# Two of four score heads are turned by SBUF to SBUF DMAs instead of by way of DRAM, and the loads around them change places

## The chip, the cores and the metric

The kernel runs on one core of a Trainium2 chip. The time is the device time in microseconds; before the change its median is 3578.6 us over three runs (3576.97 to 3579.74). The engines are named as in the profile: PE multiplies matrices, PEld loads its weights, DVE, ACT and POOL work on tiles, and SP issues the DMAs.

## The reference, cut to what matters

A Perceiver layer of three blocks, 16 sequences of 128 queries each with 512 features, in float32. Only the first block touches the change: cross attention of 16 heads of 32 features over a context of 2048 rows.

```python
q = queries @ wq.T + bq
k = context @ wk.T + bk
v = context @ wv.T + bv
attn = jnp.einsum('bhnd,bhsd->bhns', q, k) * scale
attn = jax.nn.softmax(attn, axis=-1)
out = jnp.einsum('bhns,bhsd->bhnd', attn, v)
out = out.transpose(0, 2, 1, 3).reshape(B, NQ, D)
return out @ wo.T + bo
```

Behind it come a Mamba block (projections, a causal convolution, a state scan over 16 states, a gated output and an MLP) and a mixture of experts.

## The kernel before, in words

The order of the work is written out by hand: each engine, and SP's queue with it, takes its instructions in the order of the program. The main loop runs over steps u. One step of the first 256 handles one sequence b, one block of 512 context rows and one group of four heads: u = 16 b + 4 block + group. Beside that, each step carries a piece of the projections of the next block and, from u = 54 on, a piece of the Mamba scan of sequences already attended to. Four steps make one block, 32 steps one cycle of the Mamba part (two sequences).

**Scores and their turning.** `scores(u)` writes four banks of PSUM (L307), `maxima` (L315, DVE) and `exps` (L325, ACT) turn them into the tile `pr`. The product with the values needs the probabilities turned. Two of the four heads are turned by PE with an identity (`turn`, L357, copied out by ACT in L359). The other two are turned by DVE and DMAs: `blocks(u)` transposes 32 x 32 blocks into the tile `tr` (L337, one buffer) and writes it to a DRAM tile `trd` with one DMA (L341). In the next step `gathered` reads it back with four DMAs, one for each 32 partitions of the tile `pd` (L347, one buffer), so that the blocks end up in their places. `weighted` (L385) multiplies the PE-turned heads of step u - 1 and the DMA-turned heads of step u - 2 in step u.

**Keys and values.** The projections of the context are made by a scheme with seven products in place of eight. The context block lies in four quarters, loaded by `load_ctx` (L158): `c00`, `c01`, `c10`, `c11`. POOL makes four differences of them in `ctx_sums` (L236): t1 = c01 - c00, t2 = c11 - t1, t3 = c11 - c01, t4 = c10 - t2. The products (L244) run over the four steps before a block is needed: keys with u % 4 = 1 and 2, values with u % 4 = 3 and 0. In the steps with u % 4 = 1 and 3 the products are: first with c00 and c10 (`x_products`, at the head of the step), later with t2 (`y_products`, at its end). In the steps with u % 4 = 2 and 0: first with t3 and t1, later with t4 and c11. The differences are made at u % 4 = 1, t1 and t2 first. c01 has one buffer, the other quarters two; c00, c10 and c11 of the next block are loaded at u % 4 = 1, c01 at u % 4 = 2.

**SP's queue.** All loads and stores of the loop are issued by SP. In a step its order is: the four reads of `gathered` for the step before; `step_loads` (loads of x and others, and the next but one B); the write of `tr`; `later_loads` (the next C, then the weights of the Mamba and output projections, then the context quarters). B and C are rows of `bcd` broadcast to all partitions (`load_bc`, L647), each with two buffers; POOL multiplies B in (`inputs`, L698) a step ahead, and POOL and DVE multiply C in (`scan`, L735).

**The step size of the Mamba part.** `dt_second` computes e = u - 1 - e on DVE (L679) and the logarithm of u on ACT into a tile `l` of its own (L681); POOL uses it a step later (L687).

Of the kernel before, what the change touches and what calls it, by code (L numbers as in the profile page):

```python
# [8 lines left out]
FP = mybir.dt.float32  # L9
AF = mybir.ActivationFunctionType  # L10
# [5 lines left out]
P = 128  # L16
B, NQ, D, S = 16, 128, 512, 2048
H, HD = 16, 32
KC = D // P
SB = S // 512  # L20
DI, DS, DTR = 1024, 16, 32
# [4 lines left out]
GT = GB * NQ  # L26
# [5 lines left out]
ND = 2  # L32
# [4 lines left out]
def perceiver_layer(ctx: ExitStack, tc: tile.TileContext, a: dict, out: bass.AP):  # L37
    nc = tc.nc
# [19 lines left out]
    zd = [dram.tile([NQ, D], FP, tag=f"zd{b}", name=f"zd{b}") for b in range(B)]  # L58
    xnd = [dram.tile([NQ, D], FP, tag=f"xnd{b}", name=f"xnd{b}") for b in range(B)]
    bcd = [dram.tile([2 * DS, GT], FP, tag=f"bcd{g}", name=f"bcd{g}") for g in range(B // GB)]  # L60

    trd = [dram.tile([P, ND * 512], FP, tag=f"trd{i}", name=f"trd{i}") for i in range(2)]

    mv = const.tile([P, B, 2], FP, tag="mv", name="mv")
    rstd = const.tile([P, B], FP, tag="rstd", name="rstd")
# [44 lines left out]
    LAG = 22  # L110
    Z_GATES = (20, 22, 25, 34, 36, 38, 40, 50)
    NF = B // MB
    with ExitStack() as es:
# [37 lines left out]
        def load_ctx(g, names=("c00", "c10", "c11", "c01")):  # L151

            for n in names:
                j, c = int(n[1]), int(n[2])
                t = pool.tile(
                    [P, 2, 256], FP, tag=n, name=f"{n}_{g}", bufs=1 if n == "c01" else 2
                )
                nc.sync.dma_start(  # L158
                    t,
                    a["ctxT"][g // SB, g % SB][  # L160
                        :, 2 * j : 2 * j + 2, c * 256 : (c + 1) * 256
                    ],
                )
                ctx_t[g, j, c] = t
# [60 lines left out]
        def ctx_sums(g, names):  # L225
            b11, b12, b21, b22 = (ctx_t[g, j, c] for j in range(2) for c in range(2))
            for n in names:
                t = pool.tile([P, 2, 256], FP, tag=n, name=f"{n}_{g}", bufs=1)
                cfac[g, n] = t
                x, y = {  # L230
                    "t1": lambda: (b12, b11),
                    "t2": lambda: (b22, cfac[g, "t1"]),
                    "t3": lambda: (b22, b12),
                    "t4": lambda: (b21, cfac[g, "t2"]),
                }[n]()
                nc.gpsimd.tensor_tensor(t, x, y, ALU.subtract)  # L236
# [97 lines left out]
        def blocks(u):  # L334

            t = pool.tile([P, 4, ND, 4, 32], FP, tag="tr", name=f"tr{u}", bufs=1)
            nc.vector.transpose(  # L337
                t.rearrange("p c h i q -> p (h i) c q"),
                prs[u][:, NP:, :].rearrange("p h (i c k) -> p (h i) c k", i=4, c=4),
            )  # L340
            nc.sync.dma_start(trd[u % 2], t.rearrange("p c h i q -> p (c h i q)"))  # L341

        def gathered(u):

            pd = pool.tile([P, 4, ND, 4, 32], FP, tag="pd", name=f"pd{u}", bufs=1)
            for c in range(4):
                nc.sync.dma_start(  # L347
                    pd[c * 32 : (c + 1) * 32].rearrange("k a h i q -> k a (h i q)"),
                    trd[u % 2].rearrange("(a k) (c r) -> c k a r", k=32, c=4)[c],
                )  # L350
            pds[u] = pd

        def turn(u, j):
# [323 lines left out]
        def dt_second(g, ec):  # L677
            dt, e, u = dts[g, ec]
            nc.vector.scalar_tensor_tensor(e, u, 1.0, e, ALU.subtract, ALU.subtract)  # L679
            l = ssm.tile([P, GT], FP, tag="l", name="l", bufs=1)  # L680
            nc.scalar.activation(l, u, AF.Ln)  # L681
            dts[g, ec] = dt, e, l

        def dt_third(g, ec):
            dt, e, u = dts[g, ec]
# [643 lines left out]
        for u in range(last):  # L1329
            live = u < NU  # L1330
            g, r = divmod(u - 32 - LAG, 32)
            scans = 0 <= g < NG

            made, phase = divmod(u + 3, 4)
            makes = 0 < made < B * SB
            of, phase = ("k", "v")[phase // 2], phase % 2

            def step_loads():
                for f in loads.get(u, ()):
                    f()  # L1340
                load_bc(u + 2 - 32 - LAG, 0)

            def later_loads():
                load_bc(u + 1 - 32 - LAG, DS)
                for f in weights.get(u, ()):
                    f()
                if u % 4 == 1 and made + 1 < B * SB:
                    load_ctx(made + 1, ("c00", "c10", "c11"))
                if u % 4 == 2 and made + 1 < B * SB:
                    load_ctx(made + 1, ("c01",))  # L1350

            if not 1 <= u <= NU:
                step_loads()
            if u > NU:
                later_loads()
            if scans and u <= NU:
                decays(g, r, 0)
            if u > NU:
                while fed < feeds * (u - NU) // (last - 1 - NU):
                    feed(fed)  # L1360
                    fed += 1
                if scans:
                    decays(g, r, 0)
            if u == NU + 1:
                load_rows()
            if live:
                scores(u)
            if 1 <= u <= NU:
                weighted(u - 1, range(4))
                if u > 1:  # L1370
                    weighted_last(u - 2)
                weighted_out(u - 1)
                gathered(u - 1)
                step_loads()
            for f in early.get(u, ()):
                f()
            if u == NU:
                weighted(NU, range(NP, 4))
                weighted_last(u - 1)
                att.close()  # L1380
                give_back(*banks, flat(avp))
                open_ffn()
            if u == NU + 8:
                load_wex()
            for f in head.get(u, ()):
                f()
            if live:
                maxima(u)
            if makes:
                x_products(of, made, phase, pa, pc)  # L1390
            if live:
                exps(u)

            turns = ("t1", "t2", "t3", "t4") if u % 16 == 5 else ("t1", "t2")
            if makes and u % 4 == 1:
                ctx_sums(made, turns)
            for f in between.get(u, ()):
                f()
            if 0 <= u + 1 - 32 - LAG < 32 * NG:
                inputs(*divmod(u + 1 - 32 - LAG, 32))  # L1400
            if makes and u % 4 == 1 and len(turns) == 2:
                ctx_sums(made, ("t3", "t4"))
            silu_third()
            if scans:
                scan(g, r, 0)
            if live and u % 4 == 2:
                values_kept(u // 4)
            if makes:
                hold(of, made, pa, "u1")
            if scans:  # L1410
                decays(g, r, 1)
            if live:
                blocks(u)
            if makes:
                x_sums(of, made, phase, pa, pc)
            if u <= NU:
                later_loads()

            after_turns = late.get(u, ())
            free = banks[NP:]
            places = [(free + banks)[i] for i in range(len(after_turns))]
            if live and len(after_turns) > len(free):
                if u % 4 == 0:
                    places = [flat(avp), *places[:-1]]
                elif u % 2 and makes and u not in behind:
                    places[-1] = flat(pc)

            ahead = live and u % 16 in (3, 10) and len(after_turns) == 1  # L1430
            if ahead:
                after_turns[0](free[0])
                after_turns, places = (), ()
            if live:
                for j in range(NP):
                    turn(u, j)
            if scans and not (live and u % 2):
                scan(g, r, 1)
            for f in middle.get(u, ()):
                f()  # L1440
            for f, ps in zip(after_turns, places):
                if live:
                    f(ps)
                else:
                    ps = bank()
                    f(ps)
                    give_back(ps)
            if scans and live and u % 2:
                scan(g, r, 1)
            for f in after.get(u, ()):  # L1450
                f()
            for f in inner.get(u, ()):
                f()
            if makes:
                y_products(of, made, phase, pa, pc)
                y_sums(of, made, phase, pa, pc)
            for f in behind.get(u, ()):
                ps = flat(pc) if makes else banks[2] if live else bank()
                f(ps)
                if not live:  # L1460
                    give_back(ps)
            silu_second()
# [76 lines left out]
```

## Time and profile before

| What | Value |
|---|---|
| median of three runs | 3578.6 us |
| the profiled execution's own time | 3579.3 us |
| its span, first to last instruction | 3577.5 us |
| granted TensorE clock, mean | 0.995 |
| PE busy | 3518.9 us, 98% |
| DVE, POOL, ACT busy | 2672.0, 2462.7, 2285.5 us |
| DMA engines' share, 200 to 400 us | 0.47 |
| DMA engines' share, 1100 to 2800 us | 0.79 |

In the profile, "busy" is the time in which an engine executes. A list of waits gives, for each kind of instruction, the time in which its engine stood idle before it and whose work ended that idling. SP has no busy time; each of its rows is the issuing of a DMA, and the time "to landing" runs from the start of the issue until the data is there. In the timeline a row has its start, its length, the engine, the line of the kernel, the operation and the tiles written and read; x4 stands for four merged instructions.

### The profile page before, as it was taken

Reading aid. Unit: us, or ns where it says so; the run is one execution under the profiler, and the core shown is the slowest. Engines: PE = TensorE matmul, PEld = TensorE weight load, DVE = VectorE, ACT = ScalarE, POOL = GpSimd, SP = SyncE. Lnnn points to the kernel's source line nnn. Section 1 sums busy time; section 2 is a strip of 40 time slices with the busy share of each in tenths; the row PEclk is TensorE's granted clock in tenths of the full one; section 3 lists DMA queues with packets and bytes.
Section 4 is the critical chain, followed back from the end, with each engine's and each line's share of the span. In section 5 each row is a group of like instructions: output and inputs, shape, how many; then the busy total and the mean of one; then the engine's idle time right before and its main releaser. Section 6 shows DMA issues by size and latency. Waiting matters only on the chain.

```text
span 3577.5 us, 68547 instructions
## 1 busy us (share of the span) xinstructions
PE 3518.9 (98%) x24072; PEld 2638.5 (74%) x24072; DVE 2672.0 (75%) x4390; ACT 2285.5 (64%) x5672; POOL 2462.7 (69%) x2353
## 2 busy tenths in 40 slices
PE   8999999999999999999999999999999989999999
PEld 6777787778777877787778777877777756656655
DVE  4555556897889788978797879887988767668743
ACT  3555556777677766777677767776777665545422
POOL 2111214896889788978797779777987778789920
PEclk9999999999999999999999999999999999999999
DMA  4444445787788778787788778778777887676742
GB/s 146 159 148 154 159 152 193 250 265 220 254 251 268 233 253 256 252 243 247 250 257 247 231 257 265 240 224 271 254 245 224 266 300 254 219 273 245 260 173 77
DMA packets 527541, 816.79 MB, mean 228 GB/s; under 512 B 44848, under 2 KB 378960, under 8 KB 526944
## 3 DMA queue, kind: packets, MB, share of 16 engines
q1 hardware_dynamic: 526752, 811.79, 70.4%
q8 instruction: 192, 3.15, 0.3%
q14 instruction: 149, 1.22, 0.1%
q0 software_dynamic: 448, 0.63, 0.1%
HBM read 661.51 MB, written 150.73 MB: 227 GB/s over the span
## 4 chain that ended last, share of the span: by engine, by line
PE 86%; DVE 4%; POOL 4%; DMA 3%; ACT 3%; issue 1%; SPq 0%; DVEq 0%; POOLq 0%
PE pa L244 24%; PE pc L244 17%; PE bank L307 7%; PE avp L385 7%; PE bank L577 6%; PE bank L357 6%; PE bank L986 3%; PE bank L762 3%; PE bank L955 2%; PE bank L1087 2%; PE bank L515 2%; ACT pr L325 1%; POOL w L698 1%; DMA bc<-bcd 1%; PE bank L442 1%
## 5 line engine op out<-in xcount | busy, mean ns | idle before, releaser
L325 ACT ACTIVATE pr<-bank,nm 128x512 f32<-128x512 f32 x1024 | 688.5, 684 | 199.3 <-DVE nm L315 197.3
L315 DVE TENSOR_REDUCE nm<-bank 128x1 f32<-128x512 f32 x1024 | 633.8, 678 | 60.0 <-PE bank L307 59.6
L698 POOL TENSOR_TENSOR w<-dx,bc 128x512 f32<-128x512 f32 x512 | 648.1, 1287 | 30.7 <-DMA bc<-bcd 22.6
L749 POOL TENSOR_TENSOR ysum<-ysum,w 128x512 f32<-128x512 f32 x384 | 500.4, 1303 | 229.4 <-DVE hst L712 205.9
L719 ACT ACTIVATE hst<-dt,alog 128x254 f32<-128x254 f32 x918 | 442.4, 482 | 71.5 <-DVE hst L712 39.1
L337 DVE STREAM_TRANSPOSE tr<-pr 128x1024 f32<-128x1024 f32 x256 | 318.8, 1245 | 119.9 <-ACT pr L325 110.3
L735 POOL TENSOR_TENSOR w<-w,bc 128x512 f32<-128x512 f32 x256 | 329.1, 1286 | 76.6 <-DVE w L734 74.0
L385 PEld LDWEIGHTS avp<-pT,v 128*32 128x32 f32 x4096 | 204.4, 110 | 198.3 <-issue 194.2
L734 DVE TENSOR_TENSOR_SCAN w<-hst,w 128x512 f32<-128x512 f32 x256 | 309.5, 1209 | 40.0 <-ACT hst L719 33.2
L236 POOL TENSOR_TENSOR t<-c,c 128x512 f32<-128x512 f32 x128 | 164.3, 1283 | 232.3 <-PE pc L244 135.6
L359 ACT COPY pT<-bank 128x512 f32<-128x512 f32 x512 | 271.7, 581 | 48.9 <-PE bank L357 48.8
L307 PE MATMUL bank<-kt,qT 32*128 32x512 f32 x2048 | 301.3, 641 | 1.6 <-ACT pT L359 1.6
L385 PE MATMUL avp<-pT,v 128*32 128x128 f32 x4096 | 276.4, 277 | 1.5 <-ACT pT L359 1.4
L357 PE MATMUL bank<-ident,pr 128*128 128x128 f32 x2048 | 266.2, 273 | 0.8 <-ACT pr L325 0.7
L357 PEld LDWEIGHTS bank<-ident,pr 128*128 128x128 f32 x2048 | 239.1, 141 | 27.7 <-ACT pr L325 2.5
L734 DVE TENSOR_TENSOR_SCAN hst<-hst,w 128x512 f32<-128x512 f32 x203 | 247.8, 1221 | 7.1 <-ACT hst L719 7.1
L244 PE MATMUL pa<-t,ks 128*128 128x256 f32 x1024 | 248.6, 386 | 0.0
L244 PE MATMUL pa<-vs,t 128*128 128x256 f32 x1008 | 244.8, 386 | 0.0
L577 PE MATMUL bank<-zT,win 128*128 128x256 f32 x992 | 224.8, 379 | 0.0
L244 PEld LDWEIGHTS pa<-t,ks 128*128 128x128 f32 x1024 | 185.9, 190 | 36.0 <-issue 13.8
L244 PEld LDWEIGHTS pa<-vs,t 128*128 128x128 f32 x1008 | 183.0, 190 | 35.6 <-ACT hst L719 9.9
L385 PE MATMUL avp<-pd,v 128*32 128x128 f32 x3072 | 205.8, 276 | 3.2 <-DMA pd<-trd 3.2
(315 smaller groups left out, 7709.8 us busy)
## 6 DMA issues: line engine op xcount, KB each, us to landing
bc<-bcd SPq DMA_DIRECT2D x512, 512.0 KB, 5.3
trd<-tr SPq DMA_DIRECT2D x256, 512.0 KB, 3.8
pd<-trd SPq DMA_DIRECT2D x1024, 128.0 KB, 2.9
c<-in_ctxT_dram SPq DMA_DIRECT2D x256, 256.0 KB, 6.0
wf<-in_w_dram SPq DMA_DIRECT2D x124, 512.0 KB, 6.7
wqo<-in_wqkvo_dram SPq DMA_DIRECT2D x128, 256.0 KB, 6.3
win<-in_win_dram SPq DMA_DIRECT2D x128, 256.0 KB, 5.9
wout<-in_wout_dram SPq DMA_DIRECT2D x128, 256.0 KB, 6.2
```

The costliest lines, as they stand in the source:

```text
L244: nc.tensor.matmul(ps[:, r, :], l[:, kc, r * P : (r + 1) * P], m[:, kc, :], start=(i in (1, 2, 5) and r == 0 and kc == 0), stop=(r == 1 an ...
L307: nc.tensor.matmul(banks[j], qts[b][rows, hg, :], kts[u // 4, hg][rows, :], start=True, stop=True)
L315: nc.vector.tensor_reduce(stats[b][0][j][:, sb, hg : hg + 1], banks[j], AX.X, ALU.max, negate=True)
L325: nc.scalar.activation(pr[:, j, :], banks[j], AF.Exp, bias=nm[j][:, sb, hg : hg + 1], accum_out=sm[:, sb, h : h + 1],)
L357: nc.tensor.transpose(ps[:, i, :], prs[u][:, j, i * P : (i + 1) * P], ident)
L385: nc.tensor.matmul(avp[j * HD : (j + 1) * HD, v % 4, :], values(v, i, j), pts[v, j][:, i, :] if j < NP else pds[v][:, :, j - NP, i, :], st ...
L577: nc.tensor.matmul(ps, w[:, kc, :], zTs[g][:, kc, :], start=(kc == 0), stop=(kc == KC - 1))
L698: nc.gpsimd.tensor_tensor(w, dx.unsqueeze(1).to_broadcast([P, NH // 2, GT]), bcs[g * 32 + r, 0][:, i * NH // 2 : (i + 1) * NH // 2, :], AL ...
L719: nc.scalar.activation(bt(h[:, k, :])[:, :, 1:], bt(dt)[:, :, 1:], AF.Exp, scale=aneg[:, ec, n : n + 1],)
L734: nc.vector.tensor_tensor_scan(y if i else x, y, x, 0.0, ALU.mult, ALU.add)
L735: eng.tensor_tensor(w, to, bcs[g * 32 + r, DS][:, i * NH // 2 : (i + 1) * NH // 2, :], ALU.mult)
L749: nc.gpsimd.tensor_tensor(s, s, w, ALU.add)
```

## The change

In `blocks(u)`, right behind the transposes, sixteen DMAs now move `tr` into `pd` within SBUF: for each of four 32-partition blocks of the source (a) and each of four of the destination (c) one DMA of 32 rows of 1 KB. `gathered` and the DRAM tiles are gone. `pd` has two buffers.

The loads change places. C is asked for in `step_loads`, right after B, ahead of the sixteen. Of the context quarters only c11 keeps two buffers. t3 is written in place over c01. c01 of the next block is asked for at u % 4 = 0, c11 at u % 4 = 1, c00 and c10 at u % 4 = 3; all behind the sixteen and behind the weights of the step.

In `dt_second` the logarithm is written over u; the tile `l` is gone.

```diff
-    trd = [dram.tile([P, ND * 512], FP, tag=f"trd{i}", name=f"trd{i}") for i in range(2)]
...
-                    [P, 2, 256], FP, tag=n, name=f"{n}_{g}", bufs=1 if n == "c01" else 2
+                    [P, 2, 256], FP, tag=n, name=f"{n}_{g}", bufs=2 if n == "c11" else 1
...
             for n in names:
-                t = pool.tile([P, 2, 256], FP, tag=n, name=f"{n}_{g}", bufs=1)
+                if n == "t3":
+                    t = b12
+                else:
+                    t = pool.tile([P, 2, 256], FP, tag=n, name=f"{n}_{g}", bufs=1)
...
-            nc.sync.dma_start(trd[u % 2], t.rearrange("p c h i q -> p (c h i q)"))
-
-        def gathered(u):
-
-            pd = pool.tile([P, 4, ND, 4, 32], FP, tag="pd", name=f"pd{u}", bufs=1)
-            for c in range(4):
-                nc.sync.dma_start(
-                    pd[c * 32 : (c + 1) * 32].rearrange("k a h i q -> k a (h i q)"),
-                    trd[u % 2].rearrange("(a k) (c r) -> c k a r", k=32, c=4)[c],
-                )
+            pd = pool.tile([P, 4, ND, 4, 32], FP, tag="pd", name=f"pd{u}", bufs=2)
+            for a_ in range(4):
+                for c in range(4):
+                    nc.sync.dma_start(
+                        pd[c * 32 : (c + 1) * 32, a_].rearrange("k h i q -> k (h i q)"),
+                        t[a_ * 32 : (a_ + 1) * 32, c].rearrange("k h i q -> k (h i q)"),
+                    )
             pds[u] = pd
...
-            l = ssm.tile([P, GT], FP, tag="l", name="l", bufs=1)
-            nc.scalar.activation(l, u, AF.Ln)
-            dts[g, ec] = dt, e, l
+            nc.scalar.activation(u, u, AF.Ln)
+            dts[g, ec] = dt, e, u
...
                 load_bc(u + 2 - 32 - LAG, 0)
+                load_bc(u + 1 - 32 - LAG, DS)
...
             def later_loads():
-                load_bc(u + 1 - 32 - LAG, DS)
                 for f in weights.get(u, ()):
                     f()
-                if u % 4 == 1 and made + 1 < B * SB:
-                    load_ctx(made + 1, ("c00", "c10", "c11"))
-                if u % 4 == 2 and made + 1 < B * SB:
-                    load_ctx(made + 1, ("c01",))
+                names = (("c01",), ("c11",), (), ("c00", "c10"))[u % 4]
+                if u and made + 1 < B * SB:
+                    load_ctx(made + 1, names)
...
                 weighted_out(u - 1)
-                gathered(u - 1)
                 step_loads()
```

## The prediction, made before the changed kernel was run

> **What bounds the kernel now.** I read the page first: the busy shares, then PE's waits, then SP's own waits, and last the timeline of one step, because the change lies wholly on SP's queue.
>
> ```profile
> span 3577.5 us, 68547 instructions
> ...
> PE 3518.9 (98%) x24072; PEld 2638.5 (74%) x24072; DVE 2672.0 (75%) x4390; ACT 2285.5 (64%) x5672; POOL 2462.7 (69%) x2353
> ...
> pd<-trd SPq DMA_DIRECT2D x1024, 128.0 KB, 2.9
> c<-in_ctxT_dram SPq DMA_DIRECT2D x256, 256.0 KB, 6.0
> ```
>
> PE is busy for 98% and idles 59 us; a change that takes no matmul away can gain a part of that at most. The next fence is PE's list of waits, in us in total, times, longest.
>
> ```profile
> PE bank L432 <- ACT pr L325: 7.8, 6, 1.4
> PE avp L385 <- DMA pd<-trd: 6.5, 3, 3.2
> PE bank L631 <- POOL xa L625: 4.7, 6, 0.8
> ```
>
> So the transfers that the change replaces cost PE 6.5 us in all, in three places: 2.9 and 3.2 us in the last steps, 0.3 us at 1093. The rest of PE's waits the change doesn't touch. Now SP's own waits:
>
> ```profile
> SPq L341 <- DMA c<-in_ctxT_dram: 23.5, 35, 1.3
> SPq L647 <- DMA c<-in_ctxT_dram: 34.6, 49, 1.4
> ```
>
> The write of `tr` (L341) and the loads of B and C (L647) use nothing of the context, yet wait for context loads. The semaphores of SP's DMAs show why: eight take turns, and a DMA is not issued until the one eight places earlier has landed. The timeline shows a step (u = 96, scores at 1062.75) and the next:
>
> ```profile
> 1062.75 1.14 PE L307 MATMUL bank<-kt,qT 32*128 32x512 f32 x8
> ...
> 1068.31 1.25 DVE L337 STREAM_TRANSPOSE tr<-pr 128x1024 f32<-128x1024 f32 x1 [0.43 <-ACT pr L325]
> ...
> 1070.02 0.38 SPq L341 DMA_DIRECT2D trd<-tr  x1
> ...
> 1070.44 0.43 SPq L647 DMA_DIRECT2D bc<-bcd  x1
> ...
> 1072.81 1.14 PE L307 MATMUL bank<-kt,qT 32*128 32x512 f32 x8
> ...
> 1073.55 1.28 POOL L236 TENSOR_TENSOR t<-c,c 128x512 f32<-128x512 f32 x1
> ...
> 1074.90 1.27 POOL L236 TENSOR_TENSOR t<-c,t 128x512 f32<-128x512 f32 x1
> ...
> 1076.48 1.74 SPq L347 DMA_DIRECT2D pd<-trd  x4
> ...
> 1079.33 1.89 PE L244 MATMUL pa<-t,ks 128*128 128x256 f32 x8
> ```
>
> Two things are to be seen. Four DMAs back to back take 1.74 us; a lone issue is 0.32 and the median 0.43, so one follows another every 0.475 us. And the quarter c01 has a short chain behind it: POOL makes t1 from it, t2 from t1 (1076.17), and PE wants t2 at 1079.33, in that same step.
>
> **Part 1: sixteen DMAs for five.** Gone are the 512 KB write (0.34 us of SP) and four reads (1.74). Sixteen of 32 KB come, 16 x 0.475 = 7.6 us. SP is taken 5.5 us longer a step, where a step is (2888.1 - 43.1)/256 = 11.1 us; with B and C (0.95) and the other loads (about 1.8 from the issues' medians) it is taken for 10.3. The pitch is bounded below by the shortest issue of L347 plus the gap, 0.302 + 0.043 = 0.345. Above, it is landing over eight: the other 32-row DMA, dtw, lands in 5.1 us at the median, so 0.64. I take 0.475, the nearest row: dtw too has a median issue of 0.43, so fewer rows don't shorten it. What follows in later_loads is pushed behind the sixteen.
>
> At the end the two pd waits go, since pd is asked for a step earlier: -6 us; next late there are ACT's copies (0.24 us at 2874.73, 1.4 at 2897.88). In the steps before, pd has a whole step more and stays hidden. PE has to wait for eight semaphores in place of four: its EVENT_SEMAPHORE is 51 ns, so 0 to 256 x 4 x 0.05 = 52 us; I take 0, as they are read while eight score matmuls (1.07 us) run.
>
> **Part 2: c01 asked for one step ahead.** Before, it was asked for at u % 4 = 2, three steps ahead. Now t3 lies in its buffer until PE has read it at u % 4 = 0, and only then, behind the sixteen and the step's weights, is c01 loaded, for t1 in the next step. In the step shown the transposes end at 1069.56; the sixteen take until 1077.16; c01 lands 3.6 us later; t1 and t2 take 2.62; t2 stands at 1083.4 and PE wanted it at 1079.33. PE stalls 4.0 us. The landing is bounded by 2.9 (the shortest of the context loads) and 6.0 (their median); I take 3.6, near the short end, because the sixteen ahead are small and the 512 KB write and its reading are gone.
>
> From the end of the transposes to t2 is thus 7.6 + 3.6 + 2.6 = 13.8 us, plus weights ahead of c01: four wo (2.0), two win (1.5), eight wout (4.0). The time until PE wants t2 I read from eight such timelines, u % 32 = 0, 4, 8 ... 28: 9.8, 10.9, 13.4, 20.3, 11.8, 10.7, 16.4, 13.3. With weights 0, 2, 1.5, 1.5, 0, 2, 4, 0 the stalls are 4.0, 4.9, 1.9, 0, 2.0, 5.1, 1.4, 0.5: 19.8 us a cycle, and 50 groups make 6.25 cycles: **124 us**. The thirteen groups before u = 56 (9.8 to 10.6 us in eight, 13.2 and more in five) give **38 us**. POOL, 82% busy between 1062 and 1428, waits with PE; it had run ahead of PE and I charge nothing more.
>
> **Part 3: one `tr` buffer, read by sixteen DMAs.** The next transposes wait until the last has landed. From one to the next: 15 x 0.475 + 2.4 (shortest landing of L347) + 1.25 + some 0.1 = 10.9 us. Steps 2 to 39 last 9.7: 38 x 1.2 = 46 us, of which part 2 already stalls 31, so 15 more. In the cycle from u = 91 to 104 fourteen steps take 140.7 us against 152.6, part 2 stalls 9.4 there, 2.5 remain, 16 us over 6.25 cycles. Together **31 us**; with a landing of 2.0 nearly nothing, with 3.6 see the second rival.
>
> **Part 4: eight in flight.** Eight issues are 3.8 us, wout lands in 6.2: a burst of weights holds the queue 2.4 us. About two a cycle fall ahead of a c01 (u % 32 = 22 and 24): some 5.5 us a cycle, **35 us**; none if landing shortens, 110 if every group has one.
>
> **Parts at nothing.** C is asked for before the sixteen; its buffer is free at the latest 6.1 us into a step (POOL's L735 at u % 32 = 6 and 22), when the transposes end too: SP would have waited for those. c11 and two single quarters come two steps or more ahead. Ln in place now waits for DVE's L679, 1.95 us in most of 64 cases; behind it on ACT a copy of v ends 1.1 us before PE reads it and moves into that margin. Cover gone, it is 64 x 1.95 = 125 us; but ACT idles 36% and c01's stall comes later in the same chain, so 0.
>
> The Trainium skill, "DMA: Bandwidth & Descriptors", section "Rules for kernel authors", speaks against the change: coalesce small transfers, since under 64 KB one pays mostly overhead. [...] The row of four issues in 1.74 us that land 2.9 us after issue shows that they overlap, so the sum goes by 0.475.
>
> **Sum.** 124 + 38 + 31 + 35 - 6 = 222 us on the profiled execution's 3579.3 (span 3577.5; 0.7 above the median 3578.6): 3801, said as 3800.
>
> **Rivals.** *The loop of part 3 binds every step.* With a landing of 3.6 and a pitch of 0.5 it is 7.5 + 3.6 + 1.4 = 12.5 us; 256 x (12.5 - 11.1) = 355, and c01's stall is swallowed: 3930. For it: context loads land in 6.0. Against: DMA engines lose the 512 KB write, and are at 0.79 in the middle.
> *The mild one.* Pitch 0.345, landing 2.9: 11.0 in place of 13.8; the stalls are 1.2, 2.1 and 2.3 a cycle, 35 us, and 13 before u = 56; less 6: 3621. Against it: 732 back-to-back pairs at 0.43.
> *Not slower.* c01 is there in time, and only the pd waits go: 3573. It decides at u % 32 = 0: sixteen pitches and a landing must fit 9.8 - 2.6 = 7.2 us, with 2.9 a pitch of 0.27. No issue of L347 is that short.
>
> **How the numbers follow.** Forecast 0.60 (3680 to 3900), loop 0.16, mild 0.13, not slower 0.11. The range 3600 to 3930 leaves out the last and half the loop's, 0.19. A measurement here can tell 0.2%, 7 us: the last case splits into same 0.07 and faster 0.04; slower 0.89.
>
> **What would show it.** PE waits before L244 `t,ks` for POOL L236, some 2 to 5 us at u % 4 = 1; L236 waits for DMA of `c`; SP's sixteen take 7 to 8 us; DVE's L337 waits for DMAs; no pd wait in PE's list. Wrong if sixteen issues take under 4.5 us, or if t1 starts as early as before.

## The result: 4664 us, and the profile after

The changed kernel takes 4663.7 us (median of four runs, 4663.1 to 4670.7) against 3577.9 us before (3577.0 to 3579.7). The ratio is 1.304, with a 95% interval of 1.302 to 1.306. The direction was forecast, the size was not: +1086 us where +222 had been worked out and 3930 was the range's end.

The page of the changed kernel: the span, the busy times (us, share, instructions), the chain of work that ended last, and three rows of the DMA issues (KB each, median us to landing).

```profile
span 4661.2 us, 72193 instructions
...
PE 3829.9 (82%) x24072; PEld 2785.7 (60%) x24072; DVE 2658.2 (57%) x4390; ACT 2296.2 (49%) x5672; POOL 2456.9 (53%) x2353
...
PE 34%; SPq 22%; DMA 20%; POOL 10%; issue 7%; DVE 5%; ACT 2%; DVEq 0%; POOLq 0%
...
bc<-bcd SPq DMA_DIRECT2D x512, 512.0 KB, 6.0
pd<-tr SPq DMA_DIRECT2D x4096, 32.0 KB, 1.9
c<-in_ctxT_dram SPq DMA_DIRECT2D x256, 256.0 KB, 3.4
```

PE idles 831 us (4661.2 - 3829.9) where it idled 59: 773 us more. Its busy time, for the same 24072 matmuls, is 311 us longer (3829.9 - 3518.9). Together that is the whole growth of the span, 1084 us. In the chain SP's queue and the DMAs hold 42%; before, PE alone held 86%, in the chain of that page:

```profile
PE 86%; DVE 4%; POOL 4%; DMA 3%; ACT 3%; issue 1%; SPq 0%; DVEq 0%; POOLq 0%
```

The single transfer is not slow: the moves land 1.9 us after their issue, the context quarters 3.4 us in place of 6.0.

PE's own list of waits in the changed kernel (us in total, times, longest us):

```profile
PE pa L245 <- POOL t L237: 349.5, 54, 13.5
PE pc L245 <- DVE v L275: 110.3, 35, 8.8
...
PE avp L383 <- DMA pd<-tr: 13.9, 5, 6.2
```

The products wait for POOL's differences. The list of waits of all engines says what POOL and DVE wait for:

```profile
POOL t L237 <- DMA c<-in_ctxT_dram: 792.6, 36, 64.8
DVE tr L338 <- DMA pd<-tr: 601.0, 137, 10.3
```

Both are waits for DMAs that SP issued late. SP's queue, in the timeline (start, length, issues merged under x16 and x4), over some 50 us (u = 100 to 102):

```profile
1502.03 13.00 SPq L345 DMA_DIRECT2D pd<-tr  x16
1515.08 2.00 SPq L171 DMA_DIRECT2D wqo<-in_wqkvo_dram  x4
1517.18 0.38 SPq L156 DMA_DIRECT2D c<-in_ctxT_dram  x1
1517.65 0.89 SPq L645 DMA_DIRECT2D bc<-bcd  x2
1518.64 12.73 SPq L345 DMA_DIRECT2D pd<-tr  x16
...
1535.64 10.45 SPq L345 DMA_DIRECT2D pd<-tr  x16
```

There is hardly a hole in that queue, and the sixteen moves take 10.5 to 13.0 us of a step, not 7.6. The same stretch in the timeline of the other engines shows what hangs on it: the transposes had waited for the last burst, and the quarter of the block, which stands in the queue at 1517.18, lets POOL start at 1522.31 and PE at 1524.96.

```profile
1500.72 1.25 DVE L338 STREAM_TRANSPOSE tr<-pr 128x1024 f32<-128x1024 f32 x1 [5.10 <-DMA pd<-tr]
...
1522.31 1.26 POOL L237 TENSOR_TENSOR t<-c,c 128x512 f32<-128x512 f32 x1 [13.66 <-DMA c<-in_ctxT_dram]
...
1524.96 3.78 PE L245 MATMUL pa<-t,ks 128*128 128x256 f32 x8 [11.82 <-POOL t L237]
```

The last row has a second thing in it: those eight matmuls take 3.78 us, where the eight of the step shown of before took 1.89. They run at half clock (granted clock 0.5) after 11.8 us of idling.

One issue's price is in the views by line: the moves of the changed kernel, and the four reads that they replace in the kernel before (ns minimum / median / maximum, first and last start).

```profile
L345 SPq DMA_DIRECT2D pd<-tr x4096: 507/588/2047, 47.5 to 3984.5; - x196
```

```profile
L347 SPq DMA_DIRECT2D pd<-trd x1024: 302/430/2013, 51.7 to 2902.9; - x171
```

With the gap of 0.044 us between issues the moves follow one another every 0.633 us. Summing all issues on SP's queue, and the gaps between its instructions, each counted up to 0.1 us, from the transposes of u = 60 to those of u = 250, gives SP's own time per step:

| Kernel | step, us | DMAs | SP's own time, us | share |
|---|---|---|---|---|
| before | 11.49 | 10.1 | 5.7 | 50% |
| changed | 15.88 | 21.1 | 13.6 | 86% |

Of the 2.3 us left to SP in a step, 1.19 are waits for B or C (their DMA has to land before the one eight places later is issued) and 0.76 are waits for the transposes. Over the whole run they stand at the head of SP's own list of waits:

```profile
SPq L345 <- DVE tr L338: 280.9, 171, 17.5
SPq L345 <- DMA bc<-bcd: 237.2, 243, 2.6
```

### The profile page after: what moved, and what is told of

It is laid out like the page before. It is cut to its first block, busy times and chain, and to the rows that moved or that the text cites. A ratio compares the mean times of both kernels' runs of the same rounds, so it can differ in the third digit from the quotient of the medians.

```text
span 4661.2 us, 72193 instructions
## 1 busy us (share of the span) xinstructions
PE 3829.9 (82%) x24072; PEld 2785.7 (60%) x24072; DVE 2658.2 (57%) x4390; ACT 2296.2 (49%) x5672; POOL 2456.9 (53%) x2353
## 4 chain that ended last, share of the span: by engine, by line
PE 34%; SPq 22%; DMA 20%; POOL 10%; issue 7%; DVE 5%; ACT 2%; DVEq 0%; POOLq 0%
SPq L345 19%; DMA bc<-bcd 12%; PE pa L245 9%; PE pc L245 5%; DMA pd<-tr 3%; PE bank L308 3%; PE bank L983 2%; POOL t L237 2%; POOL w L695 2%; PE avp L383 2%; PE bank L575 2%; DMA c<-in_ctxT_dram 2%; PE bank L952 2%; PE bank L355 1%; PE bank L1084 1%
## 5 line engine op out<-in xcount | busy, mean ns | idle before, releaser
L338 DVE STREAM_TRANSPOSE tr<-pr 128x1024 f32<-128x1024 f32 x256 | 318.8, 1245 | 754.7 <-DMA pd<-tr 601.0
L237 POOL TENSOR_TENSOR t<-c,c 128x512 f32<-128x512 f32 x64 | 80.9, 1264 | 1249.0 <-DMA c<-in_ctxT_dram 792.6
L245 PE MATMUL pa<-t,ks 128*128 128x256 f32 x512 | 197.9, 553 | 349.7 <-POOL t L237 349.5
L245 PEld LDWEIGHTS pa<-t,ks 128*128 128x128 f32 x512 | 136.6, 279 | 393.9 <-POOL t L237 367.8
L308 PE MATMUL bank<-kt,qT 32*128 32x512 f32 x2048 | 360.2, 721 | 5.9 <-ACT pT L357 3.9
L575 PE MATMUL bank<-zT,win 128*128 128x256 f32 x992 | 255.7, 415 | 94.0 <-DMA win<-in_win_dram 88.9
L286 ACT COPY u2ku<-pa 128x512 f32<-128x512 f32 x64 | 37.5, 586 | 552.5 <-PE pa L245 552.4
L383 PE MATMUL avp<-pT,v 128*32 128x128 f32 x4096 | 286.0, 282 | 6.9 <-DVE v L275 6.8
L575 PEld LDWEIGHTS bank<-zT,win 128*128 128x128 f32 x992 | 203.1, 210 | 135.3 <-issue 72.2
L731 DVE TENSOR_TENSOR_SCAN hst<-hst,w 128x512 f32<-128x512 f32 x203 | 247.8, 1221 | 10.4 <-ACT hst L716 10.1
L245 PE MATMUL pc<-vs,c 128*128 128x256 f32 x504 | 156.2, 464 | 110.5 <-DVE v L275 110.3
```

The source lines that it names most:

```text
L245: nc.tensor.matmul(ps[:, r, :], l[:, kc, r * P : (r + 1) * P], m[:, kc, :], start=(i in (1, 2, 5) and r == 0 and kc == 0), stop=(r == 1 an ...
L308: nc.tensor.matmul(banks[j], qts[b][rows, hg, :], kts[u // 4, hg][rows, :], start=True, stop=True)
L383: nc.tensor.matmul(avp[j * HD : (j + 1) * HD, v % 4, :], values(v, i, j), pts[v, j][:, i, :] if j < NP else pds[v][:, :, j - NP, i, :], st ...
L575: nc.tensor.matmul(ps, w[:, kc, :], zTs[g][:, kc, :], start=(kc == 0), stop=(kc == KC - 1))
L731: nc.vector.tensor_tensor_scan(y if i else x, y, x, 0.0, ALU.mult, ALU.add)
```

## The experiments

The first set of four kernels was laid out for two theories: the loop (the transposes wait for the sixteen moves of the step before, since `tr` has one buffer, with SP's own time as a floor under it) and the late quarter c01. What it gave led to theory S: SP's issuing is itself the bound. Sixteen moves at 0.633 us are 10.1 of SP's 13.6 us, and 13.6 exceeds PE's 11.5 us a step. Its rivals in the later sets are the moved loads, the crossing of the partitions, and waits that take turns. Times are medians of four runs; the ratios are to the kernel before on the same chip (3583.6, 3583.5, 3582.9 and 3581.9 us in the four sets, 3577.9 beside the changed kernel, so differences between sets are good to some 5 us).

### One wait cured at a time

The quarter c01 ahead of the sixteen:

```diff
+            if live and u and u % 4 == 0 and made + 1 < B * SB:
+                load_ctx(made + 1, ("c01",))
             if live:
                 blocks(u)
...
-                names = (("c01",), ("c11",), (), ("c00", "c10"))[u % 4]
+                names = ((), ("c11",), (), ("c00", "c10"))[u % 4]
```

> The changed kernel with c01 asked for ahead of the sixteen in place of behind them. Theory of the loop (the next transposes wait for the sixteen to land in the one tr buffer, so a step lasts as long as the sixteen and what follows them): the steps that wait for t2 fall to the length of the others, from a mean of 15.8 to 14.1 us in 200 steps and from 13.9 to 13.0 in 48: 380 us less, 4280. Rival, the late quarter is what holds PE: nearly all of the loss goes, 3700 or less.

Two buffers for `tr` (the second edit keeps the other user of that tag in step):

```diff
-            t = pool.tile([P, 4, ND, 4, 32], FP, tag="tr", name=f"tr{u}", bufs=1)
+            t = pool.tile([P, 4, ND, 4, 32], FP, tag="tr", name=f"tr{u}", bufs=2)
...
-            t = pool.tile([P, 2 * n, 256], FP, tag=tag, name=f"{tag}{key}{g}", bufs=1)[:, 0:2, :]
+            t = pool.tile([P, 2 * n, 256], FP, tag=tag, name=f"{tag}{key}{g}", bufs=n)[:, 0:2, :]
```

> The changed kernel with two buffers for tr in place of one, so that the transposes need not wait for the sixteen of the step before. If that wait is the bound, DVE's 601 us of it go: 4060. If SP's own time is the bound beneath it (sixteen in 11.9 us, and 2.8 for the other loads of a step), a step still lasts 14.7 us and only the tail of the landing is won: 4380 to 4500. If the late quarter is the bound: 4600 to 4664.

B and C behind the sixteen:

```diff
-                load_bc(u + 2 - 32 - LAG, 0)
-                load_bc(u + 1 - 32 - LAG, DS)
 
             def later_loads():
+                load_bc(u + 2 - 32 - LAG, 0)
+                load_bc(u + 1 - 32 - LAG, DS)
```

> The changed kernel with B and C asked for behind the sixteen in place of right ahead of them. Theory of the loop: B and C take 6 us to land and, eight places on, hold up the seventh and eighth of the sixteen; the sixteen then take 10.5 us as in the steps that have no B and C, in place of 11.9: 200 x 1.4 = 280 us less, 4380. If the late quarter alone counts: 50 blocks x 1.4 = 70 us less, 4590.

Measured: 4627.8 us (ratio 1.292, 1.289 to 1.294), 4596.5 (1.283, 1.281 to 1.285) and 4687.4 (1.309, 1.307 to 1.311). Against the changed kernel that is -36, -67 and +24 us; neither the quarter nor the loop is the cause by itself. Two buffers gave, but for 4 us, what the quarter's theory said of them, and missed the 4380 to 4500 that SP's own time as the bound beneath the loop would have given; but the first run takes the late quarter itself away and gains next to nothing. There PE's wait for t2 falls from 349.5 us to 0.9, and the time goes elsewhere: DVE's wait for the moves grows from 601.0 us to 910.3, and PE's list of waits with the quarter ahead has:

```profile
PE pc L245 <- DVE kt L265: 179.7, 37, 7.3
PE pc L245 <- DVE v L275: 134.4, 37, 7.8
...
PE pa L245 <- POOL t L237: 0.9, 2, 0.6
```

SP's own time stays at 13.6, 13.6 and 13.5 us, of steps of 15.75, 15.78 and 15.92 us. The wait for t2 was the place where a late queue showed, not what made it late.

### The moved loads alone

The DRAM round trip is put back as it was (`trd`, one write, `gathered` with four reads, `pd` with one buffer); the places of the loads, the single quarters, t3 in c01 and the Ln in place stay changed.

> The changed kernel with the old way through DRAM put back (one write, four reads, one pd buffer); B and C at the head of the step, the single quarters, t3 over c01 and the logarithm in place stay. Theory of the sixteen (all of the loss comes from issuing sixteen DMAs in each step): c01 now stands behind one write of 0.34 us; from the end of the transposes to t2 it is 0.4 + weights + 3.6 + 2.6 = 6.6 us and at most 4 more, against the 9.8 us and more that PE leaves, so the time is that of before, 3565 to 3600. Rival, the moved and unbuffered loads cost by themselves: some 3 us a block of context, 64 blocks, 3770 or more.

Measured: 3772.6 us (1.052, 1.048 to 1.055). The theory that the sixteen are all of the loss fails: the moves of the loads, which the prediction had at nothing or as a consequence of the sixteen, cost 189 us without them. The next two take that apart. First, the quarter ahead, as above:

> The changed kernel with the DRAM round trip back (as in the run of the moved loads alone, 3773 us), and the quarter c01 asked for ahead of the transposes' write and the four reads. If the 189 us of the moved loads are the late quarter (the products wait 78 + 33 us for GpSimd's sums, and those 381 us for the quarters): 3590 to 3660. If they are C's load ahead of the round trip (SyncE's reads wait 824 us for the write in place of 369): it stays at 3740 to 3790.

Measured: 3699.1 us (1.033, 1.031 to 1.035). That is 74 us back, a part. Then C also at its old place, behind the write:

```diff
-                load_bc(u + 1 - 32 - LAG, DS)
 
             def later_loads():
+                load_bc(u + 1 - 32 - LAG, DS)
```

> The changed kernel with the DRAM round trip back and the quarter c01 ahead (3699 us), and C's load back at its old place behind the transposes' write. If C ahead of the round trip is the rest of the moved loads' cost (SyncE's reads wait 934 us for the write, 369 before): 3585 to 3630. If the rest is the single quarters' buffers or the Ln in place: 3680 to 3710.

Measured: 3597.8 us (1.004, 1.0025 to 1.0055); 101 us more come back, and the wait that was named goes with them. SP's own waits for the write of `tr` to land, before its reads, in the three kernels in this order:

```profile
SPq L350 <- DMA trd<-tr: 823.6, 212, 10.3
```

```profile
SPq L350 <- DMA trd<-tr: 934.0, 224, 9.6
```

```profile
SPq L350 <- DMA trd<-tr: 442.2, 206, 7.2
```

In the kernel before it is 368.9 us. So with the round trip a 512 KB load ahead of a write that somebody waits for costs 101 us, the late quarter 74, and what remains (single quarters, t3 in place, Ln in place, the quarter's new place) 15 us (9 to 20) of the 189.

### Number against crossing, bytes and landing

Four moves of 128 rows by 1 KB between the same tiles:

```diff
             for a_ in range(4):
-                for c in range(4):
-                    nc.sync.dma_start(
-                        pd[c * 32 : (c + 1) * 32, a_].rearrange("k h i q -> k (h i q)"),
-                        t[a_ * 32 : (a_ + 1) * 32, c].rearrange("k h i q -> k (h i q)"),
-                    )
+                nc.sync.dma_start(
+                    pd[:, a_].rearrange("k h i q -> k (h i q)"),
+                    t[:, a_].rearrange("k h i q -> k (h i q)"),
+                )
```

> The changed kernel, with its sixteen moves of 32 rows by 1 KB replaced by four moves of 128 rows by 1 KB: the same bytes between the same tiles, but no block crosses to other partitions (that part of the computation is left out). If SyncE's own time to issue is the bound (theory S: sixteen times 0.633 us is 10.1 us of the 13.6 us that SyncE issues in a step of 15.9 us), twelve moves fewer take about 7.6 us off SyncE's step, to some 6 us, well under the 11.5 us of TensorE's step, and the time falls to 3650 to 3800, what the moves of the loads cost alone. If it is the bytes that pass between the partitions, the landing of the moves or the one buffer of the transposes (rival), the time stays above 4300.

Eight moves of 64 rows (`pd[c * 64 : (c + 1) * 64, a_]` from `t[c * 64 : (c + 1) * 64, a_]`, c in two):

> As the sixteen moves that do not cross, with eight moves of 64 rows by 1 KB: the same bytes (the crossing is left out). Theory S: SyncE's own issuing is about 6 us a step with four and 13.6 with sixteen, so 8.5 with eight, under TensorE's 11.5: the time stays near that of four, 3660 to 3850, and does not lie a third of the way to 4660. Rival, every DMA costs the same wherever the bound is: 3670 + 4/12 x 990 = 4000.

Sixteen of 32 rows, from 32 partitions to the same 32:

> The changed kernel with each of its sixteen moves going from 32 partitions to the same 32 partitions, so that no block crosses (that part of the computation is left out); number, size, queue and place of the DMAs are unchanged. If the number of DMAs on SyncE's queue decides (theory S), 4600 to 4700 as the changed kernel. If it is the crossing between partitions (rival), it falls towards the 3670 of the four moves without crossing.

And eight with the quarter ahead:

> The run with eight moves of 64 rows (crossing left out, 3881 us), and the quarter c01 asked for ahead of them. Theory S: SyncE issues 8.1 us in a step of 12.8 and has room, so this cure works here: of the 298 us over the kernel before, the products' waits for GpSimd's sums (147 + 51 us, and the slower clock behind them) go, 3640 to 3720. Rival, the quarter's place matters no more here than with sixteen (36 us): 3830 to 3880.

| Moves a step | time, us | ratio, 95% | step, us | SP's own time, us |
|---|---|---|---|---|
| 4 | 3669.7 | 1.023 to 1.026 | 11.99 | 5.5 |
| 8 | 3881.5 | 1.082 to 1.085 | 12.83 | 8.1 |
| 8, quarter ahead | 3643.9 | 1.016 to 1.020 | 11.80 | 8.2 |
| 16, not crossing | 4674.1 | 1.302 to 1.307 | 15.87 | 13.5 |
| 16, the changed kernel | 4663.7 | 1.302 to 1.306 | 15.88 | 13.6 |

The crossing costs nothing that is seen here (4674.1 against 4663.7), and the bytes are the same in all rows. The number alone makes 1004 us between four and sixteen. It is no price per DMA: four more cost 212 us, the next eight 793. Eight came out 32 us above the end of what theory S gave, because the late quarter, which stands behind them in the queue, weighs more than I had put it. The third row confirms that: with eight moves SP has room, and the single cure takes off 238 us; with sixteen it took off 36. The same cure works where the queue isn't full. The chain of work that ended last, with sixteen not crossing and with eight:

```profile
PE 35%; SPq 22%; DMA 22%; POOL 8%; issue 5%; DVE 4%; ACT 2%; DVEq 0%; POOLq 0%
```

```profile
PE 65%; DMA 9%; POOL 9%; SPq 5%; ACT 5%; DVE 4%; issue 4%; POOLq 0%; DVEq 0%; ACTq 0%
```

### All three cured at once, with sixteen

> The changed kernel with all three remedies at once: two buffers for the transposes, the quarter c01 ahead of the sixteen, B and C behind them. Theory S (SyncE's own issuing, 12.3 + 1.2 us of every step with scans, cannot be hidden): the step stays at 13.6 us or above, the time at 4250 to 4600. Rival, the waits take turns and each hides the next: with all three gone the step goes back towards TensorE's 11.5 us, 3650 to 3900.

Measured: 4473.8 us (1.249, 1.247 to 1.251), as theory S had it, and 190 us under the changed kernel. SP's own time is 13.5 of 15.39 us. PE's wait for t2 is gone but for 4.6 us, and DVE's for the moves too. In their place, in the list of all engines' waits, B and C come late, since they now stand behind the sixteen:

```profile
POOL w L695 <- DMA bc<-bcd: 978.5, 176, 11.7
DVE w L732 <- DMA bc<-bcd: 475.4, 121, 9.4
```

So whatever stands last in the full queue is what somebody waits for. What this doesn't show is a step that runs at SP's own 13.6 us: none of the kernels with sixteen moves on SP came under 15.39. Nor is it a clean test of the rival: of the three remedies, B and C behind the moves had cost 24 us alone and makes the new waits here, while the two that had gained weren't run together without it. By SP's sums the surplus over PE's 11.5 us is some 2.1 us of issuing, which stays in whatever order the DMAs are issued, and about 2 us of waits, which move when they are cured.

### The sixteen alone, and on two queues

The kernel before with the sixteen moves where its four reads stood (end of the step), all else as before:

> The kernel before with one edit: no DRAM round trip, and at the place of its four reads (end of a step) the sixteen moves from the transposes' tile; all loads, buffers and the Ln's tile as before. Theory S: SyncE issues 5.7 us a step in the kernel before; five DMAs of about 0.45 us go and sixteen of 0.633 come, 13.5 us, which is again above TensorE's 11.5 us, so 4300 to 4660. Rival, the sixteen are harmful only together with the moved loads (late quarter, C ahead): 3600 to 3900.

Measured: 5416.2 us (1.512, 1.509 to 1.514), worse than either theory had. The moves stand behind PE's products with the values (`pd` has one buffer here), `tr` has one buffer, and the next transposes have to wait for the last of them. DVE's row in the list of waits:

```profile
DVE tr L335 <- DMA pd<-tr: 2101.2, 234, 13.9
```

The step is 18.7 us. This is the loop of the prediction's rival, in a place where it does bind: the sixteen no longer run beside the rest of the step. The run shows that the moves don't need the moved loads to do harm; it says nothing on SP's bound.

The changed kernel with half of its moves issued by ScalarE:

```diff
-                    nc.sync.dma_start(
+                    (nc.scalar if c % 2 else nc.sync).dma_start(
```

> The changed kernel, with eight of its sixteen moves issued by ScalarE in place of SyncE. Theory S: SyncE's issuing falls by 8 x 0.633 = 5.1 us, to some 8.5 us a step, under TensorE's 11.5; ScalarE, busy 8.9 us a step, takes up to 5 us more for issuing, 13.9 us, so ScalarE may become the bound: 3800 to 4250. Rival, the landing of the moves or the one buffer of the transposes: same DMAs, same bytes, 4550 to 4700.

Measured: 4591.5 us (1.282, 1.280 to 1.284). That is the rival's number, but not for the rival's reason. SP's own time falls to 8.3 us of 15.5, and it now waits 1626 us for the transposes. ACT, in the list of waits, comes to its copies of the turned heads only when its share of the moves has been issued:

```profile
ACT pT L357 <- DMA pd<-tr: 1354.9, 242, 8.2
```

Most of this is ACT's own issuing, which doesn't count as busy: between u = 60 and 250 it fills 805 of the 966 us of these waits. In that stretch ACT computes for 8.3 us of a step, issues for 4.9 and has 0.8 of gaps (each counted up to 0.1 us): 13.9 us of 15.5. The scores wait for those copies, the transposes for the scores. The bound moved from SP to ACT. My expectation had ACT at up to 13.9 us, which is what it came to, and left out that its issues stand ahead of work that PE waits for.

The Trainium skill, "DMA: Bandwidth & Descriptors", section "Rules for kernel authors", says that DMAs from several engines share the same DMA engines and that spreading them saves only the issue time of the sequencer. This run agrees: SP's issuing fell by 5.3 us a step; the issue time was then ACT's.

### The price of one issue by its form

At the end of the kernel before, behind its last work, bursts of sixteen equal DMAs:

```diff
+        for k in range(16):
+            nc.sync.dma_start(tb[hi, 0:256], ta[lo, 0:256])
+        for k in range(16):
+            nc.sync.dma_start(tb[hi, 0:256], td[lo, 0:256])
...
+        for k in range(16):
+            nc.sync.dma_start(tb[hi, 0:64], ta[lo, 0:64])
```

> The kernel before, and at its end, behind the last of its work, bursts of sixteen equal DMAs on SyncE's queue: 32 rows by 1 KB from SBUF to SBUF, from DRAM to SBUF and from SBUF to DRAM, then 128 rows by 1 KB and 32 rows by 256 bytes from SBUF to SBUF. Theory: the issue of one goes by its form, 0.59 us and 0.63 us from one to the next between SBUF tiles in an idle queue too, 0.43 and 0.475 to or from DRAM. Rival: it is the busy queue or the landing that makes them slow, and all forms take the same 0.45 to 0.5 us here.

Measured in a single run, the views by line of the four forms that matter, SBUF to SBUF with 32 rows of 1 KB, DRAM to SBUF with the same, SBUF to SBUF with 128 rows of 1 KB, and SBUF to SBUF with 32 rows of 256 bytes (ns minimum / median / maximum):

```profile
L1476 SPq DMA_DIRECT2D form<-form x16: 507/507/611, 3575.6 to 3602.5; - x16
```

```profile
L1478 SPq DMA_DIRECT2D form<-formd x16: 302/303/339, 3604.3 to 3629.3; - x16
```

```profile
L1482 SPq DMA_DIRECT2D form<-form x16: 464/465/535, 3652.1 to 3681.3; - x16
```

```profile
L1484 SPq DMA_DIRECT2D form<-form x16: 507/507/565, 3683.2 to 3708.4; - x16
```

The price goes by the form: 0.507 us between SBUF tiles, 0.303 from DRAM (to DRAM 0.302), and it is the same for 1 KB and 256 bytes a row. The expected 0.59 and 0.43 are not met here. All moves of a burst write the same place, and each waited for the one before to land, so these are prices after a pause, and the pitch wasn't measured by this run. The traces of the two kernels have both cases: of the moves of the changed kernel, the 332 issued more than 0.15 us after the move before took 0.507 us at the median, the 3470 issued within 0.06 us of it 0.589; of the reads of the kernel before, 34 took 0.303 and 732 took 0.431. So an issue right behind another costs 0.08 or 0.13 us more than one after a pause, in the same kernel; other work alone doesn't make it dearer, since 0.507 is met in the midst of that work too.

## Why the prediction was wrong, step by step

**What held.** Slower, and by a late SP queue. Each of the signs named was there but for two: PE waits before the products with t2 (349.5 us in 54 places, up to 13.5 where 2 to 5 had been named), POOL for the quarters (792.6), DVE for the moves (601.0). The sixteen take 10.5 to 13.0 us, not 7 to 8; and the waits for `pd` didn't leave PE's list (13.9 us in five places, where I took off 6).

**Part 1, the step that failed: the price of sixteen issues, and no term for a queue that becomes the bound.** "Sixteen of 32 KB come, 16 x 0.475 = 7.6 us. ... with B and C (0.95) and the other loads (about 1.8 ...) it is taken for 10.3." Measured: 0.633 apiece, so 10.1 us, and 3.5 for the rest: 13.6 us. The nearest row that I took was a DRAM to SBUF read; the form sets the price, as the bursts show, and of a move between two SBUF tiles the trace of before had none. The value lies within my own upper bound of 0.64, and here is the real fault: I carried that bound nowhere. At 0.64 my own sum is 10.2 + 2.75 = 13.0 us of SP in a step of 11.1, and 256 x 1.88 = 481 us, a time of about 4060. A queue at 10.3 of 11.1 us needed a rival in which it becomes the bound, and had none; the range ended at 3930. Even so 4060 is 600 us short; by the step's sums the rest is mostly SP's waits in the full queue (2.3 of 15.88 us a step). The landings, on which the rivals turned, weren't the fault: the moves landed in 1.9 us and the quarters in 3.4, where 2.4 and 3.6 had been taken.

**Part 2, the late quarter** (162 us). The wait is real and larger than I had it, 349.5 us; its price by itself depends on how full the queue is: 74 us with the round trip, 238 with eight moves, 36 with sixteen, where the next late thing takes its place. Adding it to other terms as if each could be taken off alone was wrong from the point at which the queue is full.

**Part 3, the one buffer** (31 us). 67 us by the run with two buffers. The loop as a rival (3930) was not the cause either.

**Part 4, eight in flight** (35 us, 0 to 110). In SP's own list of waits it is 237.2 us behind B and C, not behind weights: the order of the loads had put these two 512 KB loads eight places ahead of the seventh and eighth move in every step with scans. Moving them behind the sixteen gained nothing (+24 us), as POOL then waits for them (547.0 us).

**Parts at nothing.** C ahead cost 101 us with the round trip in the kernel; with the sixteen, B and C behind them gained nothing. The Ln in place, the single quarters and the rest are some 15 us, nearly as costed.

**What had no term.** PE's clock. PE's busy time grew by 311 us, 29% of the growth of the span; the mean granted clock fell from 0.995 to 0.915. PE was busy for 529 us at half clock, before for 26; half of the difference, some 250 us, is what the clock adds, and the rest of the 311 stays open. The row for the products with t2 shows it, mean 553 ns for a matmul that took 386. A stall can so be paid twice: the wait, and then the slow matmuls behind it. How much of the 250 us the kernel would have lost to the full queue anyway, with PE waiting in place of computing slowly, isn't shown.

## What to carry to other kernels

Add up what a queue issues in a step, at the upper end of the price of one issue, and treat the queue as an engine: when the sum passes the step of the engine that bounds the kernel, expect it to be the bound, and expect little from changing the order behind it (here between 24 us lost and 190 us won, of 1086). Take the price of an issue from DMAs of the same form (source and destination) that follow closely on one another, not from one of the same size; when a transfer was split here at equal bytes, the number of pieces cost. Test a suspected wait in a kernel where the suspected bound has been relieved: the same cure was worth 36 us under a full queue and 238 us under one with room.

## What the runs showed of the hardware

**Half clock after idling.** In the changed kernel the granted clock is at half for 791 us, in 124 spells; before, for 36 us in seven. The spells of the changed kernel last 3.41, 6.83, 10.24 or 13.65 us, multiples of one length, but for one of 2.54. By the length of PE's idle stretch in the trace of the changed kernel, a spell followed 55 of the 55 stretches of 5 us and more, 10 of 11 of 4 to 5 us, 16 of 28 of 3 to 4 us, 8 of 51 of 2 to 3 us, and 3 of 108 of 0.3 to 2 us. The Trainium skill, "TensorE: Matmul & The Clock Gate", Part 1, gives a window of about 3.4 us of idling after which the clock is halved, and as long of work until it is whole; the lengths of the spells agree with the window. The idling agrees only in part: 61 of the 124 spells began less than 3.41 us after the start of PE's last idle stretch of 0.3 us or more, so here PE didn't have to idle for a whole window. The prediction made no use of it.

**The price of issuing.** On SP's queue a DMA between SBUF tiles is issued in 0.507 us after a pause and 0.589 right behind another, one from DRAM in 0.303 and 0.431; a quarter of the bytes costs the same (0.507, after a pause). 128 rows are a little cheaper (0.465) than 32 after a pause, and no cheaper in a row of them (0.593 at the median in the run with four moves).

**Coalescing.** The same 512 KB a step in four, eight and sixteen moves: 3670, 3881 and 4674 us. The rule to coalesce from the Trainium skill, "DMA: Bandwidth & Descriptors", section "Rules for kernel authors", which the prediction had set aside, pointed the right way; by SP's sums the cost lay in the issuing, while a move landed in 1.9 us.

**Left open.** How the step splits between SP's own time and waits once the queue is full is shown only as far as the runs go (no step under 15.39 us with sixteen moves on SP), and why an issue takes 0.08 to 0.13 us more right behind another isn't shown. Whether fewer moves could carry the blocks across the partitions wasn't tried. No run beat the kernel before, where PE is busy for 98%.
